# Eight more edge rows per group, fetched on ScalarE's queue, in a two-layer graph convolution

## The chip, the cores and the metric

The kernel runs on one core of a Trainium2 chip. A core has five engines with instruction streams of their own: TensorE (PE) multiplies matrices, VectorE (DVE) and ScalarE (ACT) work elementwise, GpSimd (POOL) here issues indirect gathers, and SyncE (SP) issues plain DMA transfers. ScalarE can issue plain DMA transfers too. All transfers are carried by 16 DMA engines. The metric is the device time of one execution in microseconds (us).

## The reference

The input is x with 6250 nodes of 512 features, and 100,000 edges (src, dst), sorted by dst. All values are float32. Cut to what matters:

```python
h = relu(layernorm(x))
deg = segment_sum(ones, src);  dinv = where(deg > 0, rsqrt(deg), 0)
norm = -dinv[src] * dinv[dst]

def cheb(x, W0, W1, b):
    prop = segment_sum(x[src] * norm[:, None], dst)   # gather rows, scale, sum by dst
    return x @ W0 + prop @ W1 + b

h = cheb(h, W1_0, W1_1, b1)
h = layernorm(h) * gamma + beta
h = where(h >= 0, h, 0.01 * h)
out = x + cheb(h, W2_0, W2_1, b2)
```

The costly part of each of the two layers is the gather of 100,000 rows of 2 KB and their sums by destination; each layer has two 512 x 512 products for every node beside it.

## The kernel before

**Tiling.** The edges are cut into 782 chunks of 128. Three chunks make a unit, four units a group, so a group holds 12 chunks (the first group has one unit), and a layer has 66 groups. The nodes are cut into 49 blocks of 128 rows. For each layer a table in HBM (`tab`) holds the rows that the edges read. A chunk's 128 rows are brought into one of a ring of 55 slots of the SBUF tile `places`. PE multiplies them by a 0/1 matrix `sel` of 32 columns per unit, which adds up the rows by destination; a group's result in PSUM is copied to SBUF as `agg`, and a second product (`place`, L773) sends its rows to the block of nodes that they belong to.

**Gathers.** GpSimd brings chunks by indirect DMA, one instruction for 128 rows (`gather_to`, L550). Some chunks, named in `one_by_one`, do not pass through GpSimd: SP reads the row number of every edge into a register (`fetch_rows`, L518) and starts one DMA of 2 KB per row (L527). `fetch` takes the next 8 rows (AT_ONCE = 8) and is called twice in each group, once before and once after the sums, so SP fetches 16 rows a group, and a chunk takes eight groups. The row numbers lie in the tile `starts`, one partition per chunk; `set_starts` fills it with one DMA for each layer, since the chunks are evenly spaced. The fetched chunks of layer 0 go to spare slots of `places`, those of layer 1 to the space of the weights of layer 0 (`w` in the profile).

**Order.** PE, GpSimd and SP run in the order in which the program text emits their work; a scheduler orders DVE and ScalarE. One round of the main loop handles group g: GpSimd's gathers for freed slots; the first `fetch`; then, for a block that is complete (three of four rounds have one), `turn`: load of x (L635, layer 1) and load of h for the block after next (`load_h`, L616, AHEAD = 2, two buffers), PE's transposes of this block's h (`own`, L627) and ScalarE's copy hT (L629); the second half of the previous block's products (`second`, products L639), whose result is stored by SP (L837 or, in layer 0, L857); `place`; ScalarE's scaled copy `an` (L871). Then the sums (L740) and ScalarE's copy `agg` (L753); the second `fetch`; and the first half of the block's dense work: transposes of `an` (L879), DVE's copy aT (L881), products of hT (L639). In layer 0 the block then passes through the layer norm on DVE and ScalarE (`sd`, L846).

SP has one queue in the order of the text: rows, loads of x and h, rows, stores. A DMA starts when the ones before it in its queue have been issued and its own waits are over.

The spacing of the fetched chunks is set where `one_by_one` is built: the j-th chunk of a layer is used at least 128 (j + 1) / 16 + 2 groups after the first fetch. That gives 6 chunks in layer 0 and 7 in layer 1.

Of the kernel before, what the change touches and what calls it, by code (L numbers as in the profile page):

```python
# [13 lines left out]
AF = mybir.ActivationFunctionType  # L14
# [5 lines left out]
SP = mybir.EngineType.SP  # L20

P = 128
# [4 lines left out]
Q = 32  # L27
# [7 lines left out]
AHEAD_OF = 27  # L35
JOIN = 12
AT_ONCE = 8
PIECES = (16, 16)
ONE_BY_ONE = (7, 2)
SECOND = 32  # L40
# [396 lines left out]
def usual_path(tc, have):  # L437
    nc = tc.nc
# [9 lines left out]
    ACT = mybir.EngineType.Activation  # L448
# [5 lines left out]
    for i, r in enumerate(rows):  # L454
        some = [g for g in range(NS) if mean[g] - drift[g] <= i * P + r and mean[g + 1] + drift[g + 1] > i * P]
        inside.append(range(some[0], some[-1] + 1))
    with ExitStack() as es:
# [14 lines left out]
        one_by_one, to_fetch = {}, []  # L472
        for layer, g in enumerate(ONE_BY_ONE):
            for j in range(SECOND):
                at = g + -(-P * (j + 1) // (2 * AT_ONCE)) + 2
                if at > NS - 5:
                    break
                t = STEP * unit[at + 1] - 1
                one_by_one[layer * NC + t] = (layer * SECOND + j, R + j % 2 if layer == 0 else j % 2)
        own_rows = [sorted(k - layer * NC for k in one_by_one if k // NC == layer) for layer in range(2)]  # L480

        def set_starts():

            for layer, some in enumerate(own_rows):
                n, step = len(some), some[1] - some[0]
                assert some == [some[0] + j * step for j in range(n)]
                rows_of = slice(layer * SECOND, layer * SECOND + n)
                at, up = (pool.tile([P, D], F32, name="xt")[rows_of, :P] for _ in range(2))
                nc.sync.dma_start(starts[rows_of], bass.AP(tensor=src.tensor, offset=src.offset + some[0] * P,
                                                           ap=[[step * P, n], [1, P]]))  # L490
                nc.vector.tensor_copy(at, starts[rows_of])
                if layer:
                    nc.vector.tensor_single_scalar(up, at, float(zero_row), op=OP.is_ge)
                    nc.vector.tensor_add(at, at, up)
                nc.vector.tensor_scalar_mul(at, at, 4.0 * tab[layer].shape[1])
                nc.vector.tensor_copy(starts[rows_of], at)
# [10 lines left out]
        def fetch(layer):  # L507

            some = to_fetch[:AT_ONCE]
            del to_fetch[:AT_ONCE]  # L510
            for t in sorted({t for t, _ in some}):
                fetch_rows(layer, t, [e for of, e in some if of == t])

        def fetch_rows(layer, t, es):

            e, n = es[0], len(es)
            at = one_by_one[layer * NC + t][0]
            _, regs = nc.values_load_multi_w_load_instructions(  # L518
                starts[at : at + 1, e : e + n], engines=(SP,), min_val=0, max_val=(tab[layer].shape[0] - 1) * tab[layer].shape[1] * 4,
                skip_runtime_bounds_check_because="rows of the table")  # L520
            flat = tab[layer].bitcast(U8).rearrange("n d -> (n d)")
            w = PIECE[layer] + 1 - layer
            flat = bass.AP(tensor=flat.tensor, offset=flat.offset,
                           ap=[[1, flat.shape[0]], [PIECE[layer] * 4, PIECES[layer]], [1, w * 4]])
            to = spread(layer * NC + t)[:, :, :w].bitcast(U8)
            for j, start in enumerate(regs):
                nc.sync.dma_start(to[e + j : e + j + 1], flat[bass.ds(start, 1)])  # L527

        def slot(k):
            if k in one_by_one:  # L530
# [26 lines left out]
        def gather_ahead():  # L557

            for t in range(AHEAD_OF):
                nc.gpsimd.indirect_dma_start(  # L560
                    out=zr(1, t), out_offset=None, in_=tab[1][: zero_row + 1, :],
                    in_offset=bass.IndirectOffsetOnAxis(ap=eidx[:, t : t + 1], axis=0))
# [164 lines left out]
        def sums(layer, g, sel, chunk, cnt=None, some=None, opens=True, closes=True):  # L727

            n = len(chunk)
            if opens:  # L730
                summed[0] = psum.tile([P, D], F32, name="ps")
            ps = summed[0]
            if some is None:
                some = [(s, q) for s in range(STEP) for q in range(n) if s < len(chunk[q])]
            for s, q in some:
                rows_of = zr(layer, chunk[q][s])
                to = ps[q * Q : (q + 1) * Q, :]
                if len(rows_of.shape) > 2:
                    to = to.rearrange("p (a b) -> p a b", a=PIECES[layer])
                nc.tensor.matmul(to, sel[:, q, s, :], rows_of, start=(s == 0),  # L740
                                 stop=(s == len(chunk[q]) - 1 and (cnt is None or chunk[q][0] >= AHEAD_OF)))
            for b in range(LATE if cnt is not None else 0):
                r = rows[NB - LATE + b]
                for q in range(n):
                    if chunk[q][0] < AHEAD_OF:
                        nc.tensor.matmul(ps[q * Q : (q + 1) * Q, :], cnt[:r, b, q * Q : (q + 1) * Q],
                                         late[NB - LATE + b][:r], start=False, stop=(b == LATE - 1))
            if closes:
                wide = layer == 0 and g < SOON.stop + 2 and g % 2
                agg[g] = pool.tile([P, D], F32, name="pre" if wide else "agg", bufs=3)  # L750
                w = D // 2 if g == NS - 1 else D
                for lo in range(0, D, w):
                    nc.scalar.activation(agg[g][: n * Q, lo : lo + w], ps[: n * Q, lo : lo + w], AF.Copy)  # L753

        def spots(i, some):

# [102 lines left out]
        def turn(layer, i, left=()):  # L859

            r = rows[i]
            if layer == 1 and i not in EARLY:
                load_x(i)
            if i + AHEAD < NB:
                load(layer, i + AHEAD)
            hT = None if i in EARLY else own(layer, i)
            for k, aT in left:
                second(layer, k, aT)
            place(i, [g for g in inside[i] if i < NB - 1 or g == NS - 1])
            an = pool.tile([P, D], F32, name="an")  # L870
            nc.scalar.activation(an[:r], placed.pop(i)[:r], AF.Copy,  # L871
                                 scale=(ndeg if layer == 1 and i not in EARLY else ndinv)[:r, i : i + 1])
            return hT, an

# [87 lines left out]
        for layer in range(2):  # L962
# [4 lines left out]
            i, chosen, left = 0, {}, []  # L967
            for g in range(NS - 1):
# [18 lines left out]
                def finished():  # L987
                    at_i, rest = i, left
                    if g == NS - JOIN or inside[at_i].stop > g:
                        for k, aT in rest:  # L990
                            second(layer, k, aT)
                        rest = []
                    while inside[at_i].stop <= g:
                        due.append((at_i, turn(layer, at_i, rest)))
                        rest = []
                        at_i += 1
                    return at_i, []
# [4 lines left out]
                if g == NS - 2 and layer == 0:  # L1002
                    assert i >= NB - LATE and gathered == NC
                    gather_ahead()
                sel, chunk = chosen.pop(g) if g in chosen else choose(g)
                assert not any(t in own_rows[layer] and to_fetch and t >= to_fetch[0][0] for c in chunk for t in c)
                if layer == 0:
# [14 lines left out]
                if g < NS - 2:  # L1022
                    sums(layer, g, sel, chunk, cnt)
                    if soon:
                        i, left = finished()
                else:
                    assert len(due) == 1 and due[0][0] == NB - 3 and all(len(c) == STEP for c in chunk)
                    if layer:
                        half = [[(s, q) for s in range(STEP) for q in range(at, at + NQ // 2)] for at in (0, NQ // 2)]
                        step = [half[0][:-2], half[0][-2:], half[1]]  # L1030
                    else:
                        step = [[(s, q) for q in range(NQ)] for s in range(STEP)]
                    sums(layer, g, sel, chunk, None, step[0], True, False)
                    k, (hT, an) = due.pop()
                    aT = first_half(layer, k, hT, an, lambda: sums(layer, g, sel, chunk, None, step[1], False, False))
                    second(layer, k, aT)
                    sums(layer, g, sel, chunk, None, step[2], False, True)
# [404 lines left out]
```

## Time and profile before

| what | value |
|---|---|
| three runs | 2581.74, 2596.72, 2611.42 us; median 2596.72 |
| profiled execution, own time | 2603.48 us |
| its span in the profile | 2601.7 us |
| mean granted clock of PE | 0.829 of full speed |
| DMA | 515.96 MB, mean 198 GB/s |
| GpSimd's queue | 124080 packets, 412.42 MB, 52.8% of the 16 DMA engines' time |
| SP's queue | 111090 packets, 101.91 MB, 12.4% |
| row fetches | 768 in layer 0 (from 241.5 to 1171.3 us), 896 in layer 1 (from 1360.2 to 2499.7 us) |
| gathers by L550 | 1181 + 267 |

How to read a page of the profile: it shows one execution. A line such as `L740 PE MATMUL ps<-places,sel 128*32 128x512 f32 x3090 | 440.1, 624 | 60.8 <-issue 55.3` is a group of instructions: source line, engine, operation, output and inputs by their names in the program, count, then total busy us and mean ns of one, then the idle time of the engine just before them and what ended most of it. In the timeline the columns are start, duration, engine, line. `SPq` and `ACTq` are the queues in which SP and ScalarE issue transfers. In the view of waits a line gives the waiting work, what released it, the total in us, how often, and the longest. The releaser is inferred. PE's matmuls are pipelined and the ends of their records are modelled.

### The profile page before, as it was taken

The numbers are of one execution on the slowest core, as the hardware profiler recorded it, in microseconds if no ns is written. First come the engines' busy times: TensorE is split into PE (matmuls) and PEld (weight loads), VectorE is DVE, ScalarE is ACT, GpSimd is POOL, SyncE is SP. The second block draws the span as 40 slices with busy tenths as digits, with TensorE's granted clock in tenths as the row PEclk, the third lists the DMA queues.
The fourth block names the chain that finished last, engine by engine and source line by source line (L and its number), as shares of the span: only waits on it lengthen the run. The fifth ranks groups of instructions, "written<-read, shape, count | busy, mean of one in ns | idle before, by whom it ended". The sixth has DMA issues, their size and how long they took to land. (4 is left out here: it accounts for less than half of the span.)

```text
span 2601.7 us, 23494 instructions
## 1 busy us (share of the span) xinstructions
PE 1802.9 (69%) x6907; PEld 741.7 (29%) x6907; DVE 674.4 (26%) x1463; ACT 387.1 (15%) x703; POOL 1475.0 (57%) x1565
## 2 busy tenths in 40 slices
PE   4478487767677777567851767767777676677588
PEld 3443132222222222223320222222223232222233
DVE  5854232322322323223341111111111111111121
ACT  5763011111101111101110000000000000000000
POOL 5455656666565656565445656565566565656550
PEclk7779788889888888788975888778888787889798
DMA  9885667667676666675545666676667666767661
GB/s 346 298 281 164 195 178 208 200 196 210 187 224 178 196 179 194 180 210 175 160 141 171 199 184 215 187 218 189 200 205 215 181 210 190 218 192 229 188 205 34
DMA packets 235349, 515.96 MB, mean 198 GB/s; under 512 B 86911, under 2 KB 88698, under 8 KB 235210
## 3 DMA queue, kind: packets, MB, share of 16 engines
q0 software_dynamic: 124080, 412.42, 52.8%
q1 hardware_dynamic: 111090, 101.91, 12.4%
q8 instruction: 57, 0.93, 0.2%
q14 instruction: 82, 0.67, 0.1%
q10 hardware_dynamic: 40, 0.02, 0.0%
HBM read 475.26 MB, written 38.86 MB: 198 GB/s over the span
## 5 line engine op out<-in xcount | busy, mean ns | idle before, releaser
L550 POOL DMA_INDIRECT places<-tab,sidx x1181 | 1121.3, 949 | 774.9 <-issue 317.7
L740 PE MATMUL ps<-places,sel 128*32 128x512 f32 x3090 | 440.1, 624 | 60.8 <-issue 55.3
L550 POOL DMA_INDIRECT places<-tab,lidx x267 | 252.4, 945 | 176.1 <-issue 73.5
L773 PE MATMUL an_ps<-agg,there 128*128 128x512 f32 (+1 forms) x554 | 292.7, 664 | 38.8 <-issue 21.6
L639 PE MATMUL u_ps<-places,aT 128*128 128x512 f32 x384 | 213.7, 707 | 43.8 <-DVE aT L881 34.9
L639 PE MATMUL u_ps<-w,hT 128*128 128x512 f32 (+1 forms) x400 | 210.5, 667 | 45.4 <-ACT hT L629 25.5
L639 PE MATMUL u_ps<-w,aT 128*128 128x512 f32 x384 | 204.7, 683 | 49.2 <-DVE aT L881 41.2
L639 PE MATMUL u_ps<-places,hT 128*128 128x512 f32 (+2 forms) x408 | 217.4, 678 | 25.6 <-issue 13.2
L627 PE MATMUL hT_ps<-ident,h 128*128 128x128 f32 x360 | 80.2, 325 | 210.4 <-issue 157.1
L740 PEld LDWEIGHTS ps<-places,sel 128*32 128x32 f32 x3090 | 99.9, 113 | 361.5 <-issue 322.9
L681 DVE TENSOR_TENSOR sel<-dlx,nodes_ps 128x384 f32<-128x384 f32 (+3 forms) x134 | 72.3, 541 | 479.8 <-remote 368.7
L753 ACT ACTIVATE agg<-ps 128x512 f32<-128x512 f32 (+2 forms) x130 | 76.1, 587 | 799.1 <-remote 537.0
L773 PEld LDWEIGHTS an_ps<-agg,there 128*128 128x128 f32 (+1 forms) x554 | 114.0, 214 | 182.4 <-issue 162.0
L879 PE MATMUL hT_ps<-ident,an 128*128 128x128 f32 x384 | 74.6, 325 | 116.1 <-issue 54.8
L840 DVE TENSOR_TENSOR u_ps<-u_ps,bias 128x512 f32<-128x512 f32 x45 | 31.5, 700 | 444.2 <-PE ps L740 146.5
L834 DVE SCALAR_TENSOR_TENSOR u_ps<-u_ps,root,bias 128x512 f32<-128x512 f32 x45 | 34.2, 759 | 423.0 <-remote 147.1
L629 ACT ACTIVATE hT<-hT_ps 128x512 f32<-128x512 f32 (+1 forms) x98 | 58.2, 594 | 556.2 <-remote 188.6
L627 PEld LDWEIGHTS hT_ps<-ident,h 128*128 128x128 f32 x360 | 49.8, 161 | 281.5 <-issue 278.9
L639 PEld LDWEIGHTS u_ps<-places,aT 128*128 128x128 f32 x384 | 85.1, 231 | 157.2 <-issue 106.6
L639 PEld LDWEIGHTS u_ps<-w,aT 128*128 128x128 f32 x384 | 82.4, 223 | 154.8 <-issue 104.4
L639 PEld LDWEIGHTS u_ps<-places,hT 128*128 128x128 f32 (+1 forms) x408 | 87.6, 226 | 120.6 <-issue 108.0
L639 PEld LDWEIGHTS u_ps<-w,hT 128*128 128x128 f32 (+1 forms) x400 | 82.7, 218 | 134.0 <-issue 107.0
(201 smaller groups left out, 1273.1 us busy)
## 6 DMA issues: line engine op xcount, KB each, us to landing
h<-tab SPq DMA_DIRECT2D x90, 256.0 KB
places<-tab,sidx POOLq DMA_INDIRECT x1181
w<-tab SPq DMA_DIRECT2D x896, 2.0 KB
places<-tab SPq DMA_DIRECT2D x768, 2.1 KB
xt<-in_x_dram SPq DMA_DIRECT2D x48, 256.0 KB
out_dram<-t SPq DMA_DIRECT2D x48, 256.0 KB
tab<-t SPq DMA_DIRECT2D x46, 256.0 KB
tab<-places SPq DMA_DIRECT2D x22, 528.0 KB
```

The costliest lines, as they stand in the source:

```text
L550: nc.gpsimd.indirect_dma_start(out=places[:, slot(t), :] if own_scale else zr(layer, t), out_offset=None, in_=x if layer == 0 and t < RAW ...
L627: nc.tensor.transpose(ps[:, kc, :r], h[:r, kc * P : (kc + 1) * P], ident[:r, :r])
L629: nc.scalar.activation(hT[:, :, :r], ps[:, :, :r], AF.Copy)
L639: nc.tensor.matmul(u_ps[:r], hT[:, kc, :r], w[:, kc, :], start=(start and kc == 0), stop=(stop and kc == KD - 1))
L681: nc.vector.tensor_tensor(sel[:, q : q + k, :w, :], of, node[:, q : q + k, None, :].to_broadcast([P, k, w, Q]), op=OP.is_equal)
L740: nc.tensor.matmul(to, sel[:, q, s, :], rows_of, start=(s == 0), stop=(s == len(chunk[q]) - 1 and (cnt is None or chunk[q][0] >= AHEAD_OF)))
L753: nc.scalar.activation(agg[g][: n * Q, lo : lo + w], ps[: n * Q, lo : lo + w], AF.Copy)
L773: nc.tensor.matmul(placed[i][:r], t[:m, :r], agg[g][:m, :], start=(g == inside[i][0]), stop=(g == inside[i][-1]))
L834: nc.vector.scalar_tensor_tensor(v, v, root[:r, i : i + 1], bias2[:r], op0=OP.mult, op1=OP.add)
L840: nc.vector.tensor_add(v, v, pre.pop(i)[:r] if i in EARLY else bias1[:r])
L879: nc.tensor.transpose(ps[:, kc, :r], an[:r, kc * P : (kc + 1) * P], ident[:r, :r])
```

## The change

A new constant, a new spacing, and a second fetcher:

```diff
+TO_ACT = 4
...
-                at = g + -(-P * (j + 1) // (2 * AT_ONCE)) + 2
+                at = g + -(-P * (j + 1) // (3 * AT_ONCE)) + 2
...
             for layer, some in enumerate(own_rows):
-                n, step = len(some), some[1] - some[0]
-                assert some == [some[0] + j * step for j in range(n)]
+                n = len(some)
...
-                nc.sync.dma_start(starts[rows_of], bass.AP(tensor=src.tensor, offset=src.offset + some[0] * P,
-                                                           ap=[[step * P, n], [1, P]]))
+                for j, t in enumerate(some):
+                    k = layer * SECOND + j
+                    nc.sync.dma_start(starts[k : k + 1], src[t * P : (t + 1) * P].rearrange("(o e) -> o e", o=1))
...
             for t in sorted({t for t, _ in some}):
-                fetch_rows(layer, t, [e for of, e in some if of == t])
-
-        def fetch_rows(layer, t, es):
+                for to, row in rows_at(layer, t, [e for of, e in some if of == t], SP):
+                    nc.sync.dma_start(to, row)
+
+        held, acted = [], {}
+
+        def fetch_more(layer, ins):
+
+            if not held and len(to_fetch) < AT_ONCE:
+                return
+            with tc.issue_after(ins.ins):
+                if not held:
+                    some = to_fetch[:AT_ONCE]
+                    del to_fetch[:AT_ONCE]
+                    assert len({t for t, _ in some}) == 1
+                    held.extend(rows_at(layer, some[0][0], [e for _, e in some], ACT))
+                for to, row in held[:TO_ACT]:
+                    nc.scalar.dma_start(to, row)
+                del held[:TO_ACT]
+
+        def rows_at(layer, t, es, engine):
...
-                starts[at : at + 1, e : e + n], engines=(SP,), min_val=0, max_val=(tab[layer].shape[0] - 1) * tab[layer].shape[1] * 4,
+                starts[at : at + 1, e : e + n], engines=(engine,), min_val=0, max_val=(tab[layer].shape[0] - 1) * tab[layer].shape[1] * 4,
...
-            for j, start in enumerate(regs):
-                nc.sync.dma_start(to[e + j : e + j + 1], flat[bass.ds(start, 1)])
+            return [(to[e + j : e + j + 1], flat[bass.ds(start, 1)]) for j, start in enumerate(regs)]
...
-                    nc.scalar.activation(agg[g][: n * Q, lo : lo + w], ps[: n * Q, lo : lo + w], AF.Copy)
+                    acted[0] = nc.scalar.activation(agg[g][: n * Q, lo : lo + w], ps[: n * Q, lo : lo + w], AF.Copy)
...
-            nc.scalar.activation(an[:r], placed.pop(i)[:r], AF.Copy,
+            acted[1] = nc.scalar.activation(an[:r], placed.pop(i)[:r], AF.Copy,
...
+                if g < NS - 2 and 1 in acted:
+                    fetch_more(layer, acted[1])
                 sel, chunk = chosen.pop(g) if g in chosen else choose(g)
...
                     sums(layer, g, sel, chunk, cnt)
                     if soon:
                         i, left = finished()
+                    fetch_more(layer, acted[0])
```

`fetch` on SP stays as it was, 16 rows a group. `fetch_more` takes eight more rows a group from the same list: ScalarE loads their eight row numbers into registers and starts four transfers after its copy `an` and the other four after its copy `agg`. The order of ScalarE's work is tied to those copies with `issue_after`. With 24 rows a group a chunk is complete in 5.33 groups, so layer 0 has 9 such chunks and layer 1 has 10; GpSimd issues 6 gathers fewer. As the chunks are no longer evenly spaced, `set_starts` brings their row numbers with one transfer for each chunk, 19 in place of 2. Nothing changes in what is computed.

## The prediction

> **What bounds the kernel now.** I read the page's engine shares and costliest groups first, then the waits by engine, then the timeline of three groups of layer 1 with a window table, and last SP's own queue, because the change puts row fetches behind work on ScalarE.
>
> ```profile
> PE 1802.9 (69%) x6907; PEld 741.7 (29%) x6907; DVE 674.4 (26%) x1463; ACT 387.1 (15%) x703; POOL 1475.0 (57%) x1565
> ...
> L550 POOL DMA_INDIRECT places<-tab,sidx x1181 | 1121.3, 949 | 774.9 <-issue 317.7
> ```
>
> ```profile
> ACT agg L753 <- remote: 537.0, 49, 62.8
> ...
> POOL places L550 <- PE ps L740: 252.8, 45, 18.1
> ...
> PE hT_ps L627 <- DMA h<-tab: 53.0, 12, 10.9
> ```
>
> The columns of the second fence are total, times and longest wait in us. GpSimd's gathers wait for PE's sums (252.8 us in 45 waits): a gather needs the slot of a chunk that PE has finished. So the work that the change takes from GpSimd is taken from an engine that already waits for PE. PE itself waits in 12 places, 53.0 us, for a block's 128 rows h, which SP loads.
>
> ```profile
> 2064.77 0.66 PE L879 MATMUL hT_ps<-ident,an 128*128 128x128 f32 x4
> ...
> 2065.26 3.60 PE L639 MATMUL u_ps<-places,hT 128*128 128x512 f32 x8
> ...
> 2069.43 3.70 PE L639 MATMUL u_ps<-places,aT 128*128 128x512 f32 x8 [0.57 <-issue]
> ...
> 2069.63 0.95 POOL L550 DMA_INDIRECT places<-tab,sidx  x1 [0.30 <-issue]
> ...
> 2081.02 0.71 PE L627 MATMUL hT_ps<-ident,h 128*128 128x128 f32 x4
> ...
> 2085.87 2.78 PE L740 MATMUL ps<-places,sel 128*32 128x512 f32 x24
> ```
>
> ```profile
> 2090.90 0.69 ACT L871 ACTIVATE an<-an_ps,ndeg 128x512 f32<-128x512 f32 x1 [5.13 <-remote]
> ...
> 2100.74 0.60 ACT L753 ACTIVATE agg<-ps 128x512 f32<-128x512 f32 x1 [9.15 <-remote]
> ...
> 2100.76 0.94 POOL L550 DMA_INDIRECT places<-tab,sidx  x1 [3.42 <-remote]
> ```
>
> The columns are start, duration, engine, line. The sums' records begin at 2085.87, but what they release (agg's copy and GpSimd's next gather) starts at 2100.74 and 2100.76 together. PE's records run ahead of what it has finished, so I read the end of a group of sums from agg. From `an`, released as the sums begin, to agg are 9.8 us. PE is the pace; GpSimd stood 3.42 us waiting for it and needs 0.95 + 0.30 = 1.25 us a gather.
>
> After agg, until the next block's transposes of h (L627), PE has the transposes of `an` (0.66) and the products with hT (3.60): **4.3 us of cover**. An h that lands later than 4.3 us after the sums end holds PE, and with it everything that follows.
>
> **SP's queue before.**
>
> ```profile
> 916.18 19.79 SPq L527 DMA_DIRECT2D places<-tab  x16
> 937.37 0.01 SPq L616 DMA_DIRECT2D h<-tab  x1
> 937.45 10.56 SPq L527 DMA_DIRECT2D places<-tab  x16
> ```
>
> ```profile
> 2067.22 16.26 SPq L527 DMA_DIRECT2D w<-tab  x16
> 2083.53 0.58 SPq L635 DMA_DIRECT2D xt<-in_x_dram  x1
> 2084.20 0.38 SPq L616 DMA_DIRECT2D h<-tab  x1
> ```
>
> ```profile
> 937.40:948.10 10.70, 9.97 (x38) 4.41 (x42) 3.55 (x9) 2.21 (x4) 0.46 (x1) 0.81 0.04 5
> 916.10:936.00 19.90, 7.99 (x13) 3.23 (x13) 5.95 (x14) 2.04 (x4) 11.51 (x13) 0.62 0.67 191
> 2067.20:2083.50 16.30, 12.31 (x43) 4.25 (x42) 2.33 (x5) 0.60 (x1) 10.25 (x11) 0.94 0.71 226
> ```
>
> Sixteen row fetches, with the register loads among them, take 10.56, 16.26 or 19.79 us, so 0.66, 1.02 or 1.24 us a row. The window table (busy us of PE, PEld, DVE, ACT, GpSimd, then granted clock and the DMA engines' share) tells which: 0.66 with GpSimd idle (0.46 us busy), the others with 11 to 13 gathers beside it. An h load costs SP 0.38 and stands behind the rows.
>
> ```profile
> 938.13 1.09 PE L627 MATMUL hT_ps<-ident,h 128*128 128x128 f32 x4 [9.25 <-DMA h<-tab]
> 939.01 4.80 PE L639 MATMUL u_ps<-w,aT 128*128 128x512 f32 x8
> ```
>
> ```profile
> 2269.16 3.45 DMA h<-tab
> ```
>
> ```profile
> SPq L527 <- DMA w<-tab: 31.2, 32, 1.5
> ```
>
> PE stood 9.25 us until an h issued at 937.37 had landed at 938.13: 0.76 us on idle DMA engines. The chain of waits has one of 3.45 us. The last fence shows that a row fetch waits for landings of earlier row fetches.
>
> **What the change does to the queues.** Both programs as built number their SP and ScalarE transfers in turn over the same eight completion counters, and each transfer waits until the one that had its counter before, eight places earlier, has landed. Before, all eight belong to SP, and the wait is short. After, ScalarE's rows take counters between SP's. SP's rows are emitted early but stand in the queue behind ScalarE's of two groups later. For the h load of round 10 of layer 1, which PE wants right after the sums of round 11, the built order reads:
>
> ```
> ScalarE: agg(11) -> row 1, 2, 3, 4
> SP:      round 9, row 15   waits for ScalarE's row 1 after agg(11)
>          round 9, row 16, out store, round 10, 16 rows, load of x
>          load of h          (20 transfers after the wait)
> PE:      own(round 12)      waits for this h
> ```
>
> Row 1 cannot start before agg(11), the end of the very sums after which PE wants h. The order repeats every four groups, since three of four groups close a block. I call this place (a): 12 times in layer 1 with 20 transfers, 10 times in layer 0 with 19, once there with 12. A second place (c) has 3 transfers between (11 times in layer 1) or 1 (10 times in layer 0). The third h of each cycle has a whole group to spare and costs nothing.
>
> **The sum.** For (a) in layer 1, from the end of the sums: agg 0.60; ScalarE's row 1.02 (not shown before: SP's loaded rate, between 0.66 and 1.24); its landing 2.1, the middle of 0.76 and 3.45; 20 transfers; h's issue 0.38; h's landing. PE's sums have just freed a group of slots, so GpSimd gathers for 11 x 1.25 = 13.8 us and stops: 13 transfers at 1.02 (13.3), 7 at 0.66 (4.6), and h lands on quiet engines, 0.76. Together 0.60 + 1.02 + 2.1 + 17.9 + 0.38 + 0.76 = 22.7, less 4.3 of cover: **18.4 us of PE idle**. Layer 0, one transfer fewer: 17.8. With 12 transfers all lie under gathers: 0.60 + 1.02 + 2.1 + 12.2 + 0.38 + 3.45 - 4.3 = 15.5. Sum (a): 12 x 18.4 + 10 x 17.8 + 15.5 = **414**.
>
> (c): 0.60 + 1.02 + 2.1 + 3 x 1.02 + 0.38 + 3.45 - 4.3 = 6.3, with one transfer 4.3. Sum 11 x 6.3 + 10 x 4.3 = **112**.
>
> The clock:
>
> ```profile
> 2047.30:2057.60 10.30, 4.15 (x8) 2.26 (x9) 0.69 (x1) 0.60 (x1) 4.21 (x5) 0.50 0.64 206
> 2058.00:2066.00 8.00, 8.00 (x40) 3.07 (x39) 1.78 (x5) 0.85 (x2) 2.02 (x3) 1.00 0.15 34
> ```
>
> After waiting, PE works at 0.50 until it has been busy for a while, then at 1.00. The wait at 938.13 shows the price: transposes of 1.09, not 0.71, products of 4.80, not 3.70, 1.5 us in all; 22 times, **33**.
>
> Given back: the 53.0 us of waits for h, which the new ones replace. Six gathers fewer save GpSimd 6 x 1.25 = 7.5 us, none on the path while it waits for PE.
>
> ScalarE's own cost: per group 8 rows and a register load.
>
> ```profile
> L518 SPq TENSOR_LOAD <-low_of x208: 2/528/1472, 240.6 to 2490.8; - x104
> ```
>
> With the load's median of 0.53 that is 8 x 1.02 + 0.53 = 8.7 us, half after `an` and half after agg. The half after `an` lies beside 9.8 us of sums; the other 4.1 beside 4.3 us of cover, before the next copy of hT. I cost it at nothing; at 1.24 it would show 1.2 a group (4 x 1.24 + 0.53 - 4.3), some 110 groups, 130 us. Changing two loads of row numbers into 19 takes 17 x 0.38 = 6 us of SP once, ahead of the first fetch, and is hidden by the groups before it.
>
> Against the profiled execution: span 2601.7, own time 2603.48 (median of the runs 2596.72, 7 less). 2603 + 414 + 112 + 33 - 53 = 3109, so **3110 us**. Low end: all rows at 0.66 and landings of 0.76 make (a) 12.1, 11.4 and 6.8, together 266, (c) 9, no clock term: 2825. High end: 1.24 and 3.45 make (a) 29.6, 28.4 and 19.7, 659 together, (c) 8.5 and 6.1, 155, nothing given back: 2603 + 659 + 155 + 33 = 3450.
>
> **Rivals.** *The gathers give it back.* If the tail of each group's sums waits for gathers, GpSimd, running on while PE idles, shortens the next groups.
>
> ```profile
> 2077.35 0.11 PEld L740 LDWEIGHTS ps<-places,sel 128*32 128x32 f32 x1 [2.07 <-DMA places<-tab,sidx]
> 2078.13 0.59 PE L740 MATMUL ps<-places,sel 128*32 128x512 f32 x1 [1.68 <-issue]
> ```
>
> The 2.07 speaks for it; against it, records of PE run ahead, and GpSimd stood waiting for PE 3 us later. At 2.07 + 1.68 in three groups of each of 23 cycles it returns 259: 2850. Chance 0.12.
>
> *Nothing.* ScalarE is 15% busy, GpSimd waits for PE, SP keeps its 16 rows: if SP's fetches run so far ahead that the waits on ScalarE's rows are past when h is wanted, only the cover moves: 2600. The order above speaks against it. Chance 0.05. The Trainium skill ("DMA: Bandwidth & Descriptors", section "Issuing engines are not separate DMA queues") says that starting transfers from several engines only saves the issuing time and that all share the same 16 DMA engines; by that page alone the result would be this one. No trace here shows rows from ScalarE yet.
>
> *Faster.* GpSimd's last gathers of a group decide when the sums end, wherever SP's h load comes in time. Then 6 gathers at 1.25 and the 53.0 us go: 2603 - 7.5 - 53 = 2543. It decides from the point where SP passes (a) before agg, that is, if SP leads ScalarE by at least 20 transfers; SP's rows of 10 to 20 us in an 18 us group leave no such lead. Chance 0.04.
>
> *ScalarE alone.* No wait across queues shows, but its rows delay hT and agg: the 130 us above, 2735. Chance 0.04.
>
> **Numbers.** My forecast has 0.75. A measurement of this kernel tells about 1% from no change. Faster by more: 0.04; within: 0.05; slower: 0.91. The range takes in most of the forecast's bounds and most of the first rival: 2770 to 3380.
>
> **What would show it.** In the trace after, PE's waits before L627's transposes (their line will differ) should hold some 500 us, in two lengths, near 18 and near 5; agg-to-agg times should show one long, one middling and two short groups in each four; SP's rows should wait on transfers issued by ScalarE; GpSimd should be idle for longer; the granted clock should fall. If SP's rows show no waits on ScalarE's, or h is issued ahead of agg at (a), the argument is wrong from its first step; if the waits are there but near 12 or 28 us, a row's rate or landing was mis-sized.

## The result

| | time, us | against the kernel before |
|---|---|---|
| before | 2598.31 median of 6 (2581.74 to 2611.42) | |
| changed | 3105.82 median of 6 (3097.33 to 3115.22) | 1.1975 [1.1926, 1.2023] |
| changed, profiled execution | 3097.33, span 3095.5 | |

The change makes the kernel a fifth slower, close to the forecast of 3110. Between the profiled executions lie 3097.33 - 2603.48 = 494 us.

The page after, engine shares and two of the costliest groups:

```profile
PE 1775.0 (57%) x6907; PEld 737.1 (24%) x6907; DVE 680.1 (22%) x1466; ACT 390.3 (13%) x703; POOL 1468.7 (47%) x1559
...
L567 POOL DMA_INDIRECT places<-tab,sidx x1175 | 1114.8, 949 | 1171.5 <-PE ps L757 620.2
L644 PE MATMUL hT_ps<-ident,h 128*128 128x128 f32 x360 | 90.2, 374 | 857.8 <-DMA h<-tab 620.1
```

Every engine's busy us are what they were, to 2%; only the span has grown. PE's mean granted clock fell from 0.829 to 0.766. L644 is the line of the transposes of h (L627 before): of the 857.8 us that PE stood idle ahead of it, 620.1 were ended by a landing of h. The views of waits, of all engines and of SP's queue, with total, times and longest:

```profile
POOL places L567 <- PE ps L757: 781.6, 66, 27.4
PE hT_ps L644 <- DMA h<-tab: 620.1, 33, 26.1
```

```profile
SPq L514 <- DMA w<-tab: 168.9, 64, 10.9
```

GpSimd waits 781.6 us for PE, where it waited 252.8. PE waits 620.1 us for h, not 53.0. SP's rows wait for landings of rows up to 10.9 us long, where 1.5 was the longest in the same row of the view before. The view does not say whose rows those were; the counters below do.

One cycle of four groups of layer 1, ScalarE's timeline, the lines of agg's copy and one of the row fetches on ScalarE's queue (in brackets the engine's idle time ahead of the work, and what ended it):

```profile
1851.82 0.60 ACT L770 ACTIVATE agg<-ps 128x512 f32<-128x512 f32 x1 [2.92 <-PE hT_ps L896]
1851.90 2.57 ACTq L529 DMA_DIRECT2D w<-tab  x4
...
1889.44 0.60 ACT L770 ACTIVATE agg<-ps 128x512 f32<-128x512 f32 x1 [2.89 <-DMA w<-tab]
...
1908.16 0.60 ACT L770 ACTIVATE agg<-ps 128x512 f32<-128x512 f32 x1 [18.12 <-DMA w<-tab]
...
1926.27 0.60 ACT L770 ACTIVATE agg<-ps 128x512 f32<-128x512 f32 x1 [13.60 <-remote]
...
1949.18 0.60 ACT L770 ACTIVATE agg<-ps 128x512 f32<-128x512 f32 x1 [2.53 <-PE ps L757]
```

The groups last 37.6, 18.7, 18.1 and 22.9 us, 97.4 in all. The same four groups in the profile before:

```profile
1594.28 0.60 ACT L753 ACTIVATE agg<-ps 128x512 f32<-128x512 f32 x1 [0.20 <-remote]
1615.00 0.60 ACT L753 ACTIVATE agg<-ps 128x512 f32<-128x512 f32 x1 [2.74 <-PE hT_ps L879]
1633.61 0.60 ACT L753 ACTIVATE agg<-ps 128x512 f32<-128x512 f32 x1 [18.02 <-PE an_ps L773]
1649.37 0.60 ACT L753 ACTIVATE agg<-ps 128x512 f32<-128x512 f32 x1 [3.16 <-remote]
1668.21 0.60 ACT L753 ACTIVATE agg<-ps 128x512 f32<-128x512 f32 x1 [1.03 <-PE ps L740]
```

They last 20.7, 18.6, 15.8 and 18.8 us, 73.9 in all. So one group is long by 16.9 us and one by 4.1, the other two by 0.1 and 2.3: 23.4 us in this cycle. From all of agg's copies in the two traces: 23 groups inside the layers (10 in layer 0, 13 in layer 1) last 35 to 41 us after the change and lasted 17 to 29 before, 383 us more together; all the other groups together are 105 us longer. In the long and in the middling group of this cycle, SP's loads and PE's transposes:

```profile
1874.88 0.38 SPq L633 DMA_DIRECT2D h<-tab  x1
...
1930.37 0.38 SPq L633 DMA_DIRECT2D h<-tab  x1
```

```profile
1877.87 1.08 PE L644 MATMUL hT_ps<-ident,h 128*128 128x128 f32 x4 [22.99 <-DMA h<-tab]
...
1936.65 1.09 PE L644 MATMUL hT_ps<-ident,h 128*128 128x128 f32 x4 [13.99 <-issue]
```

In the long group the load of h is issued 23.1 us after agg (1874.88 - 1851.82) and PE goes on 3.0 us later; in the middling one 4.1 us after agg, and PE 6.3 us later. There the profile names no releaser ("issue"); that PE waits for this h is read from the order of the work. The transposes take 1.08 us and not 0.71: from 1877.9 to 1879.5 the granted clock is 0.50, from 1888 on 1.00.

The trace's record of each transfer also names its completion counter. Before, eight counters serve SP alone, but for two transfers. After, the same eight serve SP's transfers and the 810 of ScalarE. At the long group SP's row of 1854.60 waits for the counter that ScalarE's first row after agg, issued at 1851.90, had before it; the load of h of 1874.88 stands 20 transfers behind that wait. At the middling group SP's row of 1928.20 has the counter of ScalarE's first row after agg (1926.36), and h stands 3 transfers behind. These are the prediction's places (a) and (c), transfer for transfer.

### The profile page after: what moved, and what is told of

The parts are those of the page before. It is cut to its first block, busy times and chain, and to the rows that moved or that the text cites. A ratio compares the mean times of both kernels' runs of the same rounds, so it can differ in the third digit from the quotient of the medians.

```text
span 3095.5 us, 25180 instructions
## 1 busy us (share of the span) xinstructions
PE 1775.0 (57%) x6907; PEld 737.1 (24%) x6907; DVE 680.1 (22%) x1466; ACT 390.3 (13%) x703; POOL 1468.7 (47%) x1559
## 5 line engine op out<-in xcount | busy, mean ns | idle before, releaser
L644 PE MATMUL hT_ps<-ident,h 128*128 128x128 f32 x360 | 90.2, 374 | 857.8 <-DMA h<-tab 620.1
L757 PE MATMUL ps<-places,sel 128*32 128x512 f32 x3084 | 421.9, 640 | 29.0 <-issue 28.6
L790 PE MATMUL an_ps<-agg,there 128*128 128x512 f32 (+1 forms) x554 | 300.6, 677 | 60.2 <-issue 38.5
L644 PEld LDWEIGHTS hT_ps<-ident,h 128*128 128x128 f32 x360 | 57.1, 187 | 945.0 <-issue 942.4
L656 PE MATMUL u_ps<-places,hT 128*128 128x512 f32 (+2 forms) x408 | 203.4, 632 | 49.1 <-issue 38.7
L656 PE MATMUL u_ps<-w,aT 128*128 128x512 f32 x384 | 212.0, 704 | 10.4 <-DVE sel L698 3.8
L656 PE MATMUL u_ps<-w,hT 128*128 128x512 f32 (+1 forms) x400 | 199.3, 643 | 22.2 <-ACT hT L646 16.4
L757 PEld LDWEIGHTS ps<-places,sel 128*32 128x32 f32 x3084 | 97.6, 116 | 320.5 <-issue 293.9
L852 DVE TENSOR_TENSOR t<-u_ps,xt 128x512 f32<-128x512 f32 x45 | 31.0, 688 | 382.4 <-DMA xt<-in_x_dram 339.3
L656 PEld LDWEIGHTS u_ps<-places,hT 128*128 128x128 f32 (+1 forms) x408 | 79.0, 204 | 129.5 <-issue 127.3
L778 DVE TENSOR_SCALAR there<-iota_r,node_of 128x128 f32<-128x128 f32 (+1 forms) x286 | 81.3, 296 | 111.1 <-PE an_ps L790 57.8
```

Of the source, the lines that this page charges most:

```text
L644: nc.tensor.transpose(ps[:, kc, :r], h[:r, kc * P : (kc + 1) * P], ident[:r, :r])
L656: nc.tensor.matmul(u_ps[:r], hT[:, kc, :r], w[:, kc, :], start=(start and kc == 0), stop=(stop and kc == KD - 1))
L778: behind[1] = nc.vector.tensor_scalar(t[:m, :r], iota_r[:m, :r], node_of[:m, g : g + 1], -(1.0 + i * P), op0=OP.subtract, op1=OP.is_equal)
L790: nc.tensor.matmul(placed[i][:r], t[:m, :r], agg[g][:m, :], start=(g == inside[i][0]), stop=(g == inside[i][-1]))
L852: nc.vector.tensor_add(o[:r], v, own_x.pop(i)[:r])
```

## The experiments

The theory: both queues draw on one set of eight completion counters, in an order fixed when the program is built; SP's transfers stand in it behind rows that ScalarE issues later, and h (and whatever else SP carries) comes late. The rivals: 24 rows a group are more than the queues or the DMA engines carry; ScalarE's issuing holds up its copies.

The runs came in three batches of four, the first on a chip numbered 0, the other two on one numbered 15. The kernel before, run beside each batch, took 2007, 2596 and 2649 us. Ratios are against the kernel before of the same batch. Those without an interval are one run against a median; those with one are worked out from the single runs, and can differ a little from the quotient of the medians.

| kernel | rows a group, SP + ScalarE | us | before there | ratio |
|---|---|---|---|---|
| SP 8, ScalarE 16 | 24 | 2318.80 | 2006.69 | 1.154 [1.151, 1.157] |
| changed, ScalarE's rows all after an | 24 | 2387.42 | 2006.69 | 1.190 |
| changed, ScalarE's rows all after agg | 24 | 2455.62 | 2006.69 | 1.224 |
| SP 8, ScalarE 8 | 16 | 2005.50 | 2006.69 | 0.9995 [0.9985, 1.0004] |
| changed, again | 16 + 8 | 3119.02 | 2595.70 | 1.1996 [1.1944, 1.2048] |
| before, loads of h and x on GpSimd | 16 + 0 | 2704.62 | 2595.70 | 1.0448 [1.0396, 1.0500] |
| changed, the same loads on GpSimd, chunks 2 groups later | 16 + 8 | 3035.83 | 2595.70 | 1.1708 [1.1662, 1.1753] |
| changed, the same loads on GpSimd | 16 + 8 | 2997.77 | 2595.70 | 1.155 |
| SP 12, ScalarE 12 | 24 | 2683.90 | 2648.77 | 1.0113 [1.0049, 1.0177] |
| SP 12, ScalarE 8 | 20 | 2896.63 | 2648.77 | 1.094 |
| SP 8, ScalarE 8, again | 16 | 2550.93 | 2648.77 | 0.9649 [0.9591, 0.9707] |
| changed, loads ahead of SP's first rows | 16 + 8 | 3124.22 | 2648.77 | 1.179 |

### The split turned round: SP 8, ScalarE 16

```diff
-TO_ACT = 4
+TO_ACT = 8
...
                     fetch_more(layer, acted[0])
...
-                fetch(layer)
                 if layer == 0 and g == 12:
```

> The changed kernel with the split of the 24 rows a group turned round: SP fetches 8 (its fetch after the sums is left out), ScalarE 8 after an and 8 after agg. The same rows, chunks, gathers and bytes. As built, SP's load of h no longer stands behind a row that ScalarE issues in the group before h is wanted (the latest is two groups back). Theory (h is late because SP's transfers wait, counter by counter, for rows that ScalarE issues after agg): both kinds of waits for h go, and with SP relieved the old 53 us too: 2540 to 2650 us. Rival 'too many rows, or too much on the DMA engines': the same rows, so 3100. Rival 'ScalarE's issuing delays its copies': twice as many rows on ScalarE, so slower still than 3106.

Measured 1.154, a miss. No wait for h is left (one, of 3.6 us), but ScalarE now waits. Its view of waits and two lines of its timeline:

```profile
ACT agg L770 <- DMA w<-tab: 481.7, 51, 24.4
```

```profile
1737.55 23.16 ACTq L529 DMA_DIRECT2D w<-tab  x16
1760.76 0.60 ACT L770 ACTIVATE agg<-ps 128x512 f32<-128x512 f32 x1 [23.32 <-DMA w<-tab]
```

Sixteen rows took ScalarE 23.16 us, 1.45 each, where 0.64 is what four of them took in the changed kernel (2.57 / 4), and agg's copy stood behind them. It is the same coupling the other way round: by the counters in the trace, 547 of ScalarE's transfers follow one of SP's on their counter, here 4.2 us after it was issued (median), in the changed kernel 10.9 us (519). Whether ScalarE could issue sixteen rows a group without that coupling, this run does not tell, and no other does.

### Where ScalarE's rows stand: all after an, or all after agg

The same rows on the same queues, only their place differs:

```diff
-TO_ACT = 4
+TO_ACT = 8
...
-                    fetch_more(layer, acted[0])
```

and, for the other kernel, the call after `an` taken out and the call after agg kept.

> The changed kernel with all eight of ScalarE's rows after an, none after agg; SP as it is. Theory: the chain to h starts at an, 9.8 us before the sums end, but has a register load (0.5) and four transfers more (24 after ScalarE's first row, not 20); so the long waits shrink by about 5 us (23 of them, 120 us) and the short ones of 5 us vanish (21, 105 us): about 2880 us. Rivals (rows, DMA load, ScalarE's issuing, clock): nothing changes, about 3106.

> The changed kernel with all eight of ScalarE's rows after agg, none after an. Theory: the chain starts at the end of the sums with a register load and has three transfers more, so the long waits grow by about 3 us (23, 70 us), and in the short ones h waits for ScalarE's fifth row and not its first (2.6 us more, 21 times, 55 us): about 3230 us, some 350 above the kernel with the rows after an. Rivals (rows, DMA load, clock): about 3106 and no difference between the two.

Measured 2387 and 2456: the direction is the theory's, the size is not (68 us, not 350). PE's waits for h in the first and in the second:

```profile
PE hT_ps L644 <- DMA h<-tab: 540.6, 60, 19.8
```

```profile
PE hT_ps L644 <- DMA h<-tab: 643.6, 65, 21.3
```

The waits differ by 103 us. The expected times were worked out for a chip on which GpSimd waits for PE; on this one GpSimd sets the pace (next run). That part of a longer wait is then made good in the groups after it would explain the size, but is not shown. That the place matters at all speaks against the rival of the rows, whose number and bytes are the same. It does not decide about ScalarE's issuing, since the two kernels also hold up different copies: agg waits 358.5 us for rows to the tile w in the first, hT 402.4 in the second.

### Sixteen rows, 8 and 8

The first edit with TO_ACT = 4 and the spacing of before, `2 * AT_ONCE`: 13 chunks, 16 rows a group, half of them on ScalarE. It ran twice.

> Sixteen rows a group as before, 13 chunks as before, but SP fetches 8 and ScalarE 8 (SP's fetch after the sums is left out, the spacing is that of before). As built, no load of h stands behind a row of ScalarE's of the last group's end. Theory: no new waits, and the 53 us that PE waited for h before go too, since SP has half its rows: 2540 to 2600 us. Rival 'ScalarE's eight rows delay its copies' (the same eight rows at the same two places as in the changed kernel): 2735 or more.

> Sixteen rows a group, 8 on each queue, once more. Where before takes 2596 us, PE sets the pace and waits 53 us for h in the profile of before: SP with half its rows is in time, so 2540 to 2580; where before takes 2007 GpSimd sets the pace: 2005 as it was.

Measured 0.9995 and 0.9649. The engine shares of the two runs:

```profile
PE 1654.3 (83%) x6907; PEld 664.1 (33%) x6907; DVE 688.0 (34%) x1463; ACT 388.3 (19%) x703; POOL 1477.6 (74%) x1565
```

```profile
PE 1815.8 (71%) x6907; PEld 722.7 (28%) x6907; DVE 676.6 (26%) x1463; ACT 388.6 (15%) x703; POOL 1473.7 (58%) x1565
```

Two runs of the same program. In the first GpSimd is busy for 74% of the span, it waits for the sums (L757) 21.1 us in all, and its largest group of idle times,

```profile
POOL places L567 <- issue: 340.3, 1117, 0.3
```

is the 0.3 us between one gather and the next: GpSimd sets the pace, and nothing that SP gains can show. In the second GpSimd is busy for 58% and waits for the sums 163.1 us, and SP with half its rows returns 98 us against the kernel before. The 2551 us lie in the expected 2540 to 2580, but those were for a kernel before of 2596. Before was 2% slower in this batch, so how much of the 98 us, beyond the 53 that the waits for h had shown, is SP's queue stays open. ScalarE issues eight rows a group at the very places of the changed kernel, and neither run is slower: the rival "ScalarE's issuing", at eight rows, falls. This kernel beats both of the others on the chip where GpSimd waits for the sums, and equals the one before where GpSimd sets the pace.

### The changed kernel again, and SP's loads moved to GpSimd

```diff
-                nc.sync.dma_start(own_h[i][lo:hi], tab[layer][at + lo : at + hi, :D])
+                nc.gpsimd.dma_start(own_h[i][lo:hi], tab[layer][at + lo : at + hi, :D])
...
-                nc.sync.dma_start(own_x[i][lo:hi], x[i * P + lo : i * P + hi, :])
+                nc.gpsimd.dma_start(own_x[i][lo:hi], x[i * P + lo : i * P + hi, :])
```

in the kernel before, in the changed kernel, and in the changed kernel with `+ 4` for `+ 2` in the spacing.

> The changed kernel once more, beside its variants on one chip, since the kernel before took 2007 us on the chip of the last runs and 2598 on the first. There GpSimd never waits for PE, so the sums are as long as the gathers take; the queues are the same. Theory: the same two kinds of waits in each four groups (long ones of about 20 us, short ones less): between the kernels with ScalarE's rows all after an (2387) and all after agg (2456), 2400 to 2440 where before is 2007; 3106 if the chip is like the first.

> The kernel before with its loads of h and x (97 in the loop, 256 KB each) issued by GpSimd and not by SP. It is the measure of what these loads cost GpSimd. Where GpSimd sets the pace: 97 loads of about 1 to 1.25 us, so 2007 + 97 to 121, about 2110. Where PE sets the pace (before 2598): they are hidden, and the 53 us of waits for h go: about 2550.

> The changed kernel, its 16 rows on SP and 8 on ScalarE, 19 chunks, with the loads of h and x on GpSimd's queue (as in the run beside it) and each fetched chunk used two groups later (+ 4 in the spacing, not + 2), so that neither h nor a chunk stands close behind the rows that wait on ScalarE's. Theory: what was lost was h behind SP's rows, so all of it comes back: within 1% of the kernel before with the loads on GpSimd (about 2110, or 2550). Rival (24 rows a group are too much for the queues or the DMA engines, or ScalarE's rows delay its copies): as slow as the changed kernel, 2420 or more (3106).

> The same with the spacing of the changed kernel (+ 2). As built, the last rows of each fetched chunk now stand behind ScalarE's rows of the group in which the sums use them, 5 to 30 transfers after one. Theory: the waits move from h to the sums that use a fetched chunk, 19 places of about 10 us: 150 to 250 us above the run with + 4, and PE waits for rows of SP's (w or places), not for h. Rival: no difference between the two.

The changed kernel repeats its ratio. The kernel before with these loads on GpSimd, the control, costs 4.5%, not a gain of 2: GpSimd needs 0.585 us for a load of h, but it also waits in its queue for the buffers of x. The view of that line, and a line of the view of waits:

```profile
L616 POOL DMA_DIRECT2D h<-tab x90: 568/585/616, 133.6 to 2587.7; - x90
```

```profile
POOL xt L635 <- DVE t L835: 186.7, 29, 19.0
```

The kernel that should have come back to the control did not: 1.1708. Its waits:

```profile
PE u_ps L656 <- DVE t L852: 320.0, 34, 19.2
...
POOL xt L652 <- DVE t L852: 308.4, 32, 21.3
...
PE u_ps L656 <- DVE t L871: 215.6, 16, 25.5
...
ACT t L870 <- DMA tab<-t: 191.4, 14, 24.0
...
DVE t L852 <- DMA out_dram<-t: 137.0, 12, 14.7
```

PE no longer waits for h. It waits for a PSUM buffer (u_ps) that DVE frees with t, and t waits for the store of an earlier block, out_dram or tab: SP carries the stores too, behind the same rows. I had named h as the whole loss; it was only the first of SP's transfers that PE comes to need. (The changed kernel itself shows it too: DVE's t waits 339.3 us for loads of x there, 38.6 before.) With the spacing of `+ 2` the waits move to the sums as well, in its view of waits:

```profile
PE ps L757 <- DMA w<-tab: 250.7, 10, 35.1
```

so the kind was as expected, though not the total: it is 38 us below the other, not 150 to 250 above. Taking one kind of transfer off SP moves the wait to the next kind. The price falls but does not go: the kernel with `+ 4` is 331 us above its control (3035.83 - 2704.62), the changed kernel 523 above the one before. That fits the theory, and equally the rival that 24 rows are too many.

### The even split, and four rows fewer

This pair tells them apart. `fetch` and `fetch_more` take the number of rows of a call as their last argument, `fetch_more` issues all of them at once after their register load, and the spacing follows the sum.

```diff
-                fetch(layer)
+                fetch(layer, 8)
...
-                    fetch_more(layer, acted[1])
+                    fetch_more(layer, acted[1], 8)
...
-                    fetch_more(layer, acted[0])
+                    fetch_more(layer, acted[0], 4)
...
-                fetch(layer)
+                fetch(layer, 4)
```

That is SP 12, ScalarE 12. The other kernel has 4 in the call after `an`, and 20 rows a group.

> The 24 rows a group of the changed kernel, the same chunks, gathers and bytes, split evenly: SP 8 and 4, ScalarE 8 after an and 4 after agg. As built the two queues keep step: SP's load of h waits for a row that ScalarE issues a whole group before h is wanted, and ScalarE's rows wait for rows that SP issued about a group earlier. Theory (the cost is the order of the shared completion counters, in which SP's transfers stand behind ScalarE's of a later time): no waits for h, 2540 to 2620 on a chip where before takes 2596, 1990 to 2015 where it takes 2007. Rival '24 rows are too many': as slow as the changed kernel (3106; 2420). Rival 'ScalarE's issuing delays its copies': slower still, with 12 rows and not 8.

> Four rows a group fewer than the run beside it: SP 8 and 4, ScalarE 4 and 4, 20 rows a group and fewer chunks. As built, the load of h again waits for ScalarE's first row after the agg just ahead of its use, with 8 (layer 0) or 11 (layer 1) of SP's transfers after it, not 19 or 20. Theory: long waits of about 11 and 14 us, 22 of them, some 280 us, less what before waited: 2800 to 2850 (2200 where before takes 2007), so slower than the run with four rows more. Both rivals (rows, ScalarE's issuing): faster than the run with four rows more.

Measured 1.0113 and 1.094: **with four rows more, the even split is 213 us faster**. Waits for h, of the even split and of the other:

```profile
PE hT_ps L641 <- DMA h<-tab: 1.4, 1, 1.4
```

```profile
PE hT_ps L641 <- DMA h<-tab: 395.6, 24, 23.6
```

and agg's copies in one cycle of the other, ScalarE's timeline:

```profile
2209.62 0.60 ACT L767 ACTIVATE agg<-ps 128x512 f32<-128x512 f32 x1 [2.28 <-DMA w<-tab]
...
2240.89 0.60 ACT L767 ACTIVATE agg<-ps 128x512 f32<-128x512 f32 x1 [2.31 <-DMA w<-tab]
...
2257.23 0.60 ACT L767 ACTIVATE agg<-ps 128x512 f32<-128x512 f32 x1 [15.73 <-DMA w<-tab]
```

A long group of 31.3 us, then one of 16.3. The kernel with 20 rows was expected at 2800 to 2850 where before takes 2596, which is 2857 to 2908 here, and took 2897. The same rows, chunks and bytes as in the changed kernel cost 1% in place of 20%, with four rows more on ScalarE; so neither the number of rows nor ScalarE's issuing is the cause of the loss. What differs is how the queues keep step. By the counters in the traces, a transfer of SP's whose counter ScalarE had last starts 3.8 us after ScalarE's in the changed kernel (median of 517), 8.6 us in the even split (561). For ScalarE's behind SP's it is the reverse, 10.9 (519) and 3.4 us (563): in the even split it is ScalarE that follows close behind. The even split still falls short of its expectation (2540 to 2620 where before takes 2596, so 2592 to 2674 for 2649). ScalarE's copies of agg stand behind its own rows there,

```profile
ACT agg L767 <- DMA w<-tab: 403.1, 39, 19.4
```

but how much of that lies on the path was not measured.

### The loads ahead of SP's first rows

```diff
-                fetch(layer)
                 due = []
...
+                fetch(layer)
                 if g == NS - 2 and layer == 0:
                     assert i >= NB - LATE and gathered == NC
```

> The changed kernel with SP's first fetch of a round put behind the round's loads of x and h, so that 8 rows fewer of the same round stand ahead of them. As built the counters close up in the same way: 19 or 20 of SP's transfers lie between ScalarE's first row after agg and the load of h, as in the changed kernel. Theory: no gain, within 1.5% of the changed kernel (3106; about 2420). Rival (h simply stands behind the round's rows in SP's queue): 8 rows of about 0.8 us fewer in 23 places, 150 us less.

Measured 3124.22 in one run: no gain that can be told, as the theory has it (1.179, against 1.1996 of the changed kernel in the batch before; the kernel before itself differs by 2% between the two batches, so less than 2% says nothing). The rival's 150 us would be 5%. PE's waits for h stay:

```profile
PE hT_ps L644 <- DMA h<-tab: 660.6, 38, 26.2
```

So the number of rows ahead of h in the program's text is not what counts; that the place in the common order is fits the theory.

## Why the prediction was right

**The bound.** That GpSimd's share was off the path held: its waits for PE tripled. What six gathers fewer are worth, 7.5 us by the prediction, cannot be told beside 494.

**The first step, waits between the queues.** Shown: SP's rows stand on counters that ScalarE's rows after agg had just before, with 20 and 3 transfers from there to h; a cycle has one long and one middling group; and the loss follows the order of the counters from kernel to kernel (24 rows: 1.20 or 1.01; 20 rows: 1.094), not the number of rows. Not shown: that the shared counters do it and nothing else in the order of the two queues. No kernel here gives each queue counters of its own.

**The sizes.** That the total came so close is in part luck: the parts err and make it up. Per cycle of layer 1 the sum had 18.4 + 6.3 + 1.5 of clock = 26.2 us, before anything is given back; the cycle shown grew by 23.4. Over the run the 23 long groups, as many as the prediction has places (a), grew by 383 us, where (a) and the clock made 414 + 33; the rest grew by 105, where (c) less what is given back made 112 - 53.

In the long wait, h issues 23.1 us after agg; the terms up to there make 21.6. From agg to SP's waiting row it is 2.8 us (1854.60 - 1851.82), not 0.60 + 1.02 + 2.1 = 3.7: ScalarE's row starts 0.08 us after agg starts, and took 0.64, not 1.02. The 20 transfers take 20.3 us (1874.88 - 1854.60), not 17.9. From h's issue to the transposes it then takes 3.0 us, not 0.38 + 0.76: the landing on idle DMA engines was put too small, though GpSimd was idle here as well. The record that gave 0.76 is 0.01 us long, where most loads of h take 0.38, so the transfer may have begun earlier than was read. Both together make the delay 26.1 in place of 22.7. The group grew by 16.9 us all the same, and not by 26.1 - 4.3 = 21.8; the difference was not traced. The middling group grew by 4.1, not 6.3. PE's waits for h grew by 567 us, more than the 494 lost, so in part they stand in place of other idle time.

**What was given back.** The 53 us were read from PE's waits for h alone. SP with half its rows returned 98 in one batch, so SP's queue may have cost the kernel before more than those waits showed. In the changed kernel this was not separated from the new waits.

**ScalarE at nothing.** Held at eight rows a group, by the kernel with 8 and 8. At 16, and less clearly at 12, its copies wait behind its rows.

**The rivals.** "The gathers give it back" would have made 2850; the measured 3106 and GpSimd's tripled waits for PE speak against it. "ScalarE alone" falls with the kernel of 8 and 8. "Nothing" and "faster" needed SP to stay ahead of ScalarE's rows; with 8 and 8 rows PE's waits for h are gone, and 3.5% are won on one chip, none on another. The Trainium skill's rule ("DMA: Bandwidth & Descriptors", section "Issuing engines are not separate DMA queues"), that a second issuing engine saves only issuing time, fits that kernel: SP's queue, which had 10 to 20 us of rows in a group of some 18 us, is relieved of half of them, and the gain is 98 us on one chip and none on the other. The rule says nothing of the coupling that decided here.

## What to carry to other kernels

A second queue is not independent of the first if both draw on the same completion counters: read in the built program, for the transfers that the critical engine waits for, which transfer of the other queue each one waits on, and how late that one starts. Balance the queues so that they keep step; here 24 rows cost 20% when split 16 to 8 and 1% when split 12 to 12, and 16 rows split 8 to 8 gained 3.5% on one chip and nothing on another. A load moved out of a late queue helps only if everything else in that queue, stores included, has time to spare.

## What the runs showed of the hardware

The same kernel before took 2007 us on the chip numbered 0, with a mean granted clock of 0.92, and 2596 and 2649 us in the two batches on the chip numbered 15, with 0.83 and 0.82. On the first GpSimd sets the pace; on the second it waits for the sums, so the same edit (8 and 8 rows) is worth nothing on one and 3.5% on the other.

What makes the sums late on the second chip stays open. That PE itself sets the pace there is read from GpSimd's waits and from records of the sums that end some 12 us before what they release starts (2088.65 and 2100.74 in the profile before); it is not shown directly. The kernel with 8 and 8 rows ran on both: PE is busy 1654.3 us on the first and 1815.8 on the second, 10% more at a granted clock of 0.919 and 0.845, but the whole takes 28% longer. So neither the clock nor PE's recorded work accounts for the difference. A ratio is only good on the chip, and beside the kernel before, with which it was run.
